# Self attention in a decoder kernel: another order of the steps in a turn

## Chip, cores and metric

The kernel runs on one core of a Trainium2 chip. The metric is the device time of one execution in microseconds (us). A core has five engines with a queue each, worked off in order: TensorE (PE; its weight loads are shown as PEld), VectorE (DVE), ScalarE (ACT), GpSimd (POOL) and SyncE (SP), which here issues most of the transfers. An instruction that waits for another engine holds up what stands behind it on its own queue.

## The reference

The program computes a two-layer decoder on x of shape 16 x 112 x 512 (batches, positions, width) in float32. It has seven stages: an attention, a quantized self attention joined with a quantized cross attention, a mixture of experts, a second attention, a second cross attention and a gated feed-forward layer. The change lies in the quantized self attention. Of its part of the reference, this is what matters (cut):

```python
ln_out = _ln(hidden_states, ln_w, ln_b)
q = _fp8_linear_pertensor(ln_out, wq, wq_scale, q_in_scale)   # 16 heads of 128
q = _ln(q, qln_w, qln_b)
k = _ln(_fp8_linear_pertensor(ln_out, wk, wk_scale, k_in_scale), kln_w, kln_b)  # 8 of 128
v = _fp8_linear_pertensor(ln_out, wv, wv_scale, v_in_scale)
core = _gqa(q, k, v)            # softmax(q k^T / sqrt(128)) v, two query heads to a key head
...
catq = _div_clamp_fp8(cat, proj_smooth)
out = einsum(catq, wproj) * (proj_in_scale * proj_w_scale)
```

`_fp8_linear_pertensor` scales and rounds its input to 8-bit floats before the product; `_div_clamp_fp8` does the same with the attention's output.

## The kernel before, in words

The stage is `stage_fp8_self` (line 888). The heads are worked through in four quarters q (four query heads and two key heads each). A unit (`SelfUnit`, line 736) is one quarter of one batch b; there are 4 x 16 = 64 units, in the order of `self_order` (line 875): first quarter 0 mixed with quarter 1, then 2 and 3. The tokens are stored in tiles of 128 rows while a batch has 112 positions, so 14 tiles cover 16 batches: units with b = 7 and b = 15 have no tile of their own, and so no queries and no keys to project (8 units in all).

A unit goes through its steps over several turns. `turn(n)` (line 920) runs, for different units, one step of each:

- `project_q` (750) of unit n: eight matmuls into ps_q, squares on ScalarE (L745), their sum on VectorE (L746).
- `project_kv` (761) of unit n: keys and values into ps_kv, squares of the keys, a copy of the values on ScalarE (L770), then on GpSimd the reciprocal root of the variance (`rsqrt`, L491 and L492), and on VectorE the products qk (L777), which free ps_q and ps_kv.
- `transpose` (782) of unit n-1: six transposes of qk into ps_t (L792), copied on ScalarE to qt and kt by batch (L485).
- `scores` (795) of unit n-2: ps_s (L799) and the extreme of each row on VectorE (L805).
- `exponentials` (807) of unit n-2: four exponentials with their sums on ScalarE (L812), a reciprocal on VectorE (L816) and the division on GpSimd (L817), which gives pr.
- `transpose_probs` (819) of unit n-3: four transposes of pr into ps_pt (L823), copied to pt on ScalarE (L825).
- `values` (827) of unit n-3: ps_av (L831), then scaled on VectorE (L856) and rounded by `round_fp8` (L504, L505, L506, L508 on VectorE, L510 on GpSimd), which gives r_o.
- `output` (837) of unit n-4: eight matmuls into ps_acc (L648), added to the residual x on VectorE (L872).

For quarter 0 the turn also quantizes the rows of unit n+2 (`Quantized`, line 654): `transpose` (L154) into ps_xt, `scale` (L679), which makes 16 scaled pieces on ScalarE in portions, and `rounded` (L687), which rounds the queries' and keys' inputs to xq (1024 wide, L504 to L510) and the values' inputs to xv (512 wide), and writes both to memory for the later quarters (L693, L703). Other quarters load them back two turns ahead (`quantized`, 707). At a turn's end come the loads of new rows (L440), one or two pieces of later weights (`Weights.step`, 549: a load L588, centring on VectorE L572, L578, L579, scaling and copying on ScalarE L600, L601, a remainder on GpSimd L602), and in 14 turns of quarter 2 to 3 `quantize_cross` (718), four more roundings of 512 columns on VectorE and one on GpSimd. In turns -2 to 4 some products of the next stage (`EarlyKeys.product`, L637) stand at the head of the turn.

TensorE and ScalarE run in the order in which the code calls the steps (`manual_schedule`, line 967); the other queues are put in order by the scheduler of the tile framework. PSUM has three buffers "mm" for ps_q and ps_kv, one "tr" for ps_xt, and four "sc" that ps_pt, ps_t (two), ps_s, ps_acc and ps_av take in turn, in the order in which they are asked for.

Of the kernel before, what the change touches and what calls it, by code (L numbers as in the profile page):

```python
# [9 lines left out]
F32 = mybir.dt.float32  # L10
F32R = mybir.dt.float32r
# [9 lines left out]
P = 128  # L21
# [4 lines left out]
KC = D // P  # L26
# [39 lines left out]
def batches_of(t):  # L66

    b, s = divmod(t * P, S)
    return [(b, s, 0, S - s), (b + 1, 0, S - s, P - S + s)]
# [366 lines left out]
def from_positions(k, dst, src, t):  # L436

    src = src.rearrange("(s b) d -> b s d", b=B)
    for b, s, r, n in batches_of(t):
        k.nc.sync.dma_start(out=dst[r : r + n], in_=src[b, s : s + n])  # L440
# [56 lines left out]
def round_fp8(k, wk, y, parts, tag="r8"):  # L497

    nc = k.nc
    m = wk.tile(list(y.shape), BF16, tag=f"{tag}_m", name="r8_m", bufs=2)
    t = wk.tile(list(y.shape), BF16, tag=f"{tag}_t", name="r8_t", bufs=2)
    nc.vector.tensor_scalar(y, y, FP8_MAX, -FP8_MAX, ALU.min, ALU.max)  # L504
    nc.vector.tensor_scalar(m.bitcast(U16), y.bitcast(U16), 0x7F80, None, ALU.bitwise_and)  # L505
    nc.vector.tensor_scalar(m, m, 2.0**-6, 1.5 * 2.0**4, ALU.max, ALU.mult)  # L506

    nc.vector.tensor_tensor(t, y, m, ALU.add)  # L508
    for dst, tok in parts:
        nc.gpsimd.tensor_tensor(dst, t[:, :, tok], m[:, :, tok], ALU.subtract)  # L510
# [143 lines left out]
class Quantized:  # L654
# [29 lines left out]
        if self.done == 4 * KC:  # L684
            k.nc.sync.dma_start(out=k.yx_dram[self.t], in_=y)

    def rounded(self):  # L687
        k, wk = self.k, self.wk
        xq = wk.tile([P, 2, KC, P], F32R, tag="xq", name="xq", bufs=3)
        round_fp8(  # L690
            k, wk, self.y[0], [(xq.rearrange("p v c s -> p (v c) s"), slice(0, P))], "q8"
        )
        k.nc.sync.dma_start(out=k.xq_dram[self.t], in_=xq.bitcast(F32))  # L693
        parts, full = [], []
        for b, s, r, n in batches_of(self.t):
            if s == 0:
                self.xv[b] = wk.tile([P, KC, S], F32R, tag="xv", name="xv", bufs=4)
            parts.append((self.xv[b][:, :, s : s + n], slice(r, r + n)))
            if s + n == S:
                full.append(b)  # L700
        round_fp8(k, wk, self.y[1], parts, "q8")
        for b in full:
            k.nc.sync.dma_start(out=k.xv_dram[b], in_=self.xv[b].bitcast(F32))  # L703
        return xq


def quantized(k, wk, b, xv):

    xq, t = None, tile_of(b)
    if t is not None:  # L710
        xq = wk.tile([P, 2, KC, P], F32R, tag="xq", name="xq", bufs=3)
        k.nc.sync.dma_start(out=xq.bitcast(F32), in_=k.xq_dram[t])
    xv[b] = wk.tile([P, KC, S], F32R, tag="xv", name="xv", bufs=4)
    k.last_load = k.nc.sync.dma_start(out=xv[b].bitcast(F32), in_=k.xv_dram[b])
    return xq


def quantize_cross(k, wk, t):

    y = wk.tile([P, KC, P], BF16, tag="r8_y", name="r8_y", bufs=2)  # L720
    k.nc.sync.dma_start(out=y, in_=k.yx_dram[t])
    xq = wk.tile([P, 2 * KC, P], BF16, tag="y_0", name="xqx", bufs=1)
    xq = xq.rearrange("p c s -> p (c s)").bitcast(F32).rearrange("p (c s) -> p c s", c=KC)
    round_fp8(k, wk, y, [(xq, slice(0, P))])
    k.nc.sync.dma_start(out=k.xx_dram[t], in_=xq)
# [149 lines left out]
def self_order():  # L875


    order, then = [], 0
    for b in range(B):
        order.append((0, b))  # L880
        while then < (b - 7) * 11 // 8:
            order.append((1, then))
            then += 1
    order += [(1, b) for b in range(then, B)]
    return order + [(q, b) for q in (2, 3) for b in range(B)]


def stage_fp8_self(k):

    nc = k.nc
    with k.stage("s2a", mm=3, tr=1, sc=4) as wk:
        order = self_order()
        total = len(order)
        heads, xv = [Heads() for _ in range(4)], [{} for _ in range(4)]
        units = [SelfUnit(k, wk, q, b, heads[q]) for q, b in order]
        inputs = {
            n: Quantized(k, wk, units[n].tile, xv[0])
            for n, (q, b) in enumerate(order) if q == 0 and units[n].tile is not None  # L900
        }
        weights = k.next_w + [Weights(k, "self", q, wk, raw=2) for q in (1, 2, 3)]
        weights.append(Weights(k, "cross", 0, wk, raw=2))
        last = [order.index((q, B - 1)) for q in range(4)]

        def at(n):
            return units[n] if 0 <= n < total else None


        early = {-2: 3, -1: 2, 0: 2, 1: 2, 2: 3, 3: 2, 4: 2}  # L910
        then = list(range(B))

        def products(count):
            for b in then[:count]:
                if b % GB == 2 and b // GB + 2 < NB:
                    k.early.load(b // GB + 2)
                k.early.product(b)
            del then[:count]

        def turn(n):  # L920
            new = inputs.get(n + 2)
            products(early.get(n, 0))
            if new:
                new.transpose()
                new.scale(5)
            if at(n):
                units[n].project_q(weights[order[n][0]], xq.pop(n))
            if new:
                new.scale(5)
            if at(n):  # L930
                units[n].project_kv(xv[order[n][0]].pop(order[n][1]))
            if at(n - 3):
                units[n - 3].transpose_probs()
            if at(n - 1):
                units[n - 1].transpose()
            if at(n - 2):
                units[n - 2].scores()
            if new:
                new.scale(6)
            if at(n - 2):  # L940
                units[n - 2].exponentials()
            if at(n - 4):
                units[n - 4].output()
            if at(n - 3):
                units[n - 3].values()
            if new:
                xq[n + 2] = new.rounded()
            elif at(n + 2):
                q, b = order[n + 2]
                xq[n + 2] = quantized(k, wk, b, xv[q]) if q else None  # L950
            if n + 3 in inputs:
                inputs[n + 3].load()
            if 0 <= n < TILES:
                from_positions(k, k.x[:, n], k.x_dram, n)
            if n >= 3:
                weights[1].step(2)
            for q in range(3):

                if n >= last[q]:
                    count = 2 if q == 0 else 1  # L960
                    weights[q + 2].step(count, 3 if n >= last[q] + 4 else 1 + (q < 2))
            if at(n - 4) and order[n - 4][0] == 2 and units[n - 4].tile is not None:
                quantize_cross(k, wk, units[n - 4].tile)

        xq = {}
        inputs[0].load()
        with k.tc.manual_schedule(engines={mybir.EngineType.PE, mybir.EngineType.Activation}):
            for n in range(-2, total):
                turn(n)
        for n in range(total, total + 4):  # L970
            turn(n)
        k.next_w = weights[-1]
# [947 lines left out]
```

## Time and profile before

| what | value |
|---|---|
| median of 3 runs | 3947.13 us (3946.97 to 3949.84) |
| profiled execution | 3949.88 us, its span from the first to the last instruction 3948.2 us |
| mean granted clock of TensorE | 0.968 |
| busy TensorE, VectorE, ScalarE, GpSimd | 92%, 45%, 37%, 24% of the span |
| the stage of the change, first ps_xt (L154) to last ps_acc (L648) | about 296 to 1013 us |
| one ps_q group (L648, 8 matmuls 128x512) | 2.2 us |
| one exponential (L812, 112x112) | 358 ns, four a unit |
| one division (L817, 112x448, GpSimd) | 943 ns |
| the power in `rsqrt` (L492, 128x6, GpSimd) | 1341 ns |
| one copy of q or k by batch (L485) | 585 and 481 ns, two of each a unit |

In the views of a profile, a row names the line, the engine and the operation, then output<-input by the program's names. Tables of waits give in total the time that an engine stood before instructions of a line, how often, the longest, and which instruction ended the wait. In a timeline, the first number is the start in us from the span's start, the second the duration, and a bracket holds the idle time ahead of it and what ended that. The granted clock (PEclk) is the share of full speed at which TensorE was let run.

### The profile page before, as it was taken

Reading aid. Unit: us, or ns where it says so; the run is one execution under the profiler, and the core shown is the slowest. Engines: PE = TensorE matmul, PEld = TensorE weight load, DVE = VectorE, ACT = ScalarE, POOL = GpSimd, SP = SyncE. Lnnn points to the kernel's source line nnn. Section 1 sums busy time; section 2 is a strip of 40 time slices with the busy share of each in tenths; the row PEclk is TensorE's granted clock in tenths of the full one; section 3 lists DMA queues with packets and bytes.
Section 4 is the critical chain, followed back from the end, with each engine's and each line's share of the span. In section 5 each row is a group of like instructions: output and inputs, shape, how many; then the busy total and the mean of one; then the engine's idle time right before and its main releaser. Section 6 shows DMA issues by size and latency. Waiting matters only on the chain.

```text
span 3948.2 us, 46306 instructions
## 1 busy us (share of the span) xinstructions
PE 3649.8 (92%) x16482; PEld 2360.2 (60%) x16482; DVE 1781.3 (45%) x3856; ACT 1462.3 (37%) x4189; POOL 940.2 (24%) x1322
## 2 busy tenths in 40 slices
PE   7888788778799999999999999999989989999999
PEld 4445677667566566666666654555444445556788
DVE  4445767776545544454445553111243343214333
ACT  2546665445444444444444431111113341112222
POOL 2334545544322322232222220000123220000000
PEclk8999899999999999999999999999999999999999
DMA  2125323332211211121121113999930013122000
GB/s 75 56 101 173 102 91 101 113 116 88 74 56 54 73 50 50 47 72 45 51 79 48 45 35 114 296 319 317 307 124 11 1 30 118 63 71 88 11 11 17
DMA packets 118118, 364.56 MB, mean 92 GB/s; under 512 B 13280, under 2 KB 33248, under 8 KB 108848
## 3 DMA queue, kind: packets, MB, share of 16 engines
q1 hardware_dynamic: 105504, 332.20, 25.8%
q0 software_dynamic: 5040, 16.52, 1.1%
q10 hardware_dynamic: 7344, 12.89, 0.9%
q8 instruction: 131, 2.15, 0.2%
q14 instruction: 99, 0.81, 0.1%
HBM read 317.09 MB, written 44.47 MB: 92 GB/s over the span
## 4 chain that ended last, share of the span: by engine, by line
PE 67%; DVE 8%; POOL 5%; ACT 3%; issue 3%; DMA 2%; SPq 0%; ACTq 0%; POOLq 0%; DVEq 0%
PE ps_kv L1036 14%; PE ps L1385 5%; PE ps_av L1089 4%; PE ps_s L1064 3%; PE ps_y L1403 3%; PE ps_acc L648 3%; PE ps_u L1740 3%; PE ps_o L341 3%; PE ps_g L1740 3%; PE ps_q L1491 3%; PE ps_o L1722 3%; PE ps_p L1584 3%; PE ps_q L648 2%; PE ps_pt L1079 2%; PE ps L1340 2%
## 5 line engine op out<-in xcount | busy, mean ns | idle before, releaser
L1036 PE MATMUL ps_kv<-w_kv,ct 128*125 128x512 f32 x1408 | 637.4, 592 | 0.0
L1036 PEld LDWEIGHTS ps_kv<-w_kv,ct 128*125 128x125 f32 x1408 | 261.2, 187 | 277.2 <-issue 242.0
L510 POOL TENSOR_TENSOR r_o<-r_t,r_m 128x64 fp32r<-128x64 bf16 (+6 forms) x224 | 147.5, 676 | 435.7 <-DVE r_t L508 408.8
L980 ACT ACTIVATE pr<-ps_s,ex_m 112x375 f32<-112x375 f32 (+1 forms) x272 | 157.4, 579 | 161.9 <-DVE ex_m L979 151.7
L1385 PE MATMUL ps<-w_expert,xgt 128*128 128x448 f32 x560 | 216.4, 539 | 0.7 <-ACT xgt L1377 0.7
L1012 DVE TENSOR_REDUCE cu_v<-sq 125x2 f32<-125x256 f32 (+1 forms) x248 | 118.5, 478 | 181.2 <-ACT sq L1011 180.8
L233 POOL TENSOR_TENSOR pr<-pr,nq_s 112x448 f32<-112x448 f32 (+1 forms) x120 | 119.4, 996 | 323.9 <-DVE nq_s L232 249.3
L492 POOL TENSOR_TENSOR cu_v<-cu_v,mhalf 125x2 f32<-125x2 f32 (+1 forms) x248 | 190.0, 766 | 20.6
L228 ACT ACTIVATE pr<-ps_s,nq_m 112x112 f32<-112x112 f32 (+1 forms) x480 | 167.3, 373 | 58.9 <-DVE nq_m L220 54.6
L491 POOL TENSOR_SCALAR cu_v<-cu_v 125x2 f32<-125x2 f32 (+1 forms) x248 | 48.0, 194 | 581.3 <-DVE cu_v L1012 578.4
L1064 PE MATMUL ps_s<-kt,qt 128*112 128x375 f32 x512 | 183.1, 479 | 1.2 <-ACT pr L980 0.8
L979 DVE TENSOR_REDUCE ex_m<-ps_s 112x1 f32<-112x375 f32 (+1 forms) x272 | 148.5, 546 | 69.9 <-PE ps_s L1611 67.3
L1011 ACT ACTIVATE sq<-ps_kv 125x256 f32<-125x256 f32 x176 | 67.4, 383 | 272.6 <-PE ps_kv L1036 219.9
L485 ACT ACTIVATE qt<-ps_t,turned 128x448 f32<-128x448 f32 (+6 forms) x224 | 116.5, 572 | 137.9 <-PE ps_t L1048 127.3
L1089 PE MATMUL ps_av<-pt,vn 125*128 125x224 f32 x768 | 162.4, 362 | 0.0
L1385 PEld LDWEIGHTS ps<-w_expert,xgt 128*128 128x128 f32 x560 | 103.7, 190 | 91.9 <-issue 91.0
L648 PE MATMUL ps_acc<-w_self,r_o 128*128 128x512 f32 x448 | 130.0, 436 | 28.8 <-POOL r_o L510 23.6
L1079 PEld LDWEIGHTS ps_pt<-ident,pr 112*125 112x125 f32 x768 | 102.8, 189 | 89.5 <-DVE pr L1071 50.0
L242 ACT COPY ptt<-ps_pt 112x448 f32<-112x448 f32 (+1 forms) x120 | 67.3, 561 | 226.4 <-PE ps_pt L240 226.4
L1089 PEld LDWEIGHTS ps_av<-pt,vn 125*128 125x128 f32 x768 | 145.3, 194 | 8.7 <-ACT pt L1082 3.9
L1064 PEld LDWEIGHTS ps_s<-kt,qt 128*112 128x112 f32 x512 | 90.1, 177 | 99.7 <-issue 59.7
L1079 PE MATMUL ps_pt<-ident,pr 112*125 112x112 f32 x768 | 118.4, 284 | 32.4 <-DVE pr L1071 30.5
(294 smaller groups left out, 7478.2 us busy)
## 6 DMA issues: line engine op xcount, KB each, us to landing
w_expert<-in_moe_w SPq DMA_DIRECT2D x105, 896.0 KB
ct<-in_ctx_t SPq DMA_DIRECT2D x64, 750.0 KB
xq<-xq_dram SPq DMA_DIRECT2D x42, 512.0 KB
xq<-xx_dram SPq DMA_DIRECT2D x56, 256.0 KB
raw<-in_self_w SPq DMA_DIRECT2D x48, 256.0 KB
w_sum<-in_ffn_w SPq DMA_DIRECT2D x12, 1024.0 KB
cn<-in_ctx SPq DMA_DIRECT2D x16, 750.0 KB
xv<-xv_dram SPq DMA_DIRECT2D x48, 224.0 KB
```

The costliest lines, as they stand in the source:

```text
L228: nc.scalar.activation(pr[:, j, :], self.ps[:, j, r * t : (r + 1) * t], AF.Exp, bias=self.mx[r][:, j : j + 1], scale=-1.0, accum_out=sums[ ...
L492: nc.gpsimd.tensor_tensor(dst, dst, bc(k.minus_half[: dst.shape[0]], [dst.shape[0], n]), ALU.pow)
L510: nc.gpsimd.tensor_tensor(dst, t[:, :, tok], m[:, :, tok], ALU.subtract)
L648: k.nc.tensor.matmul(out, lhs(c), w[i][:, c, :], start=first and c == 0 and i == 0, stop=last and c == n - 1 and i == 1,)
L979: nc.vector.tensor_reduce(mx, src, AX.X, ALU.min)
L980: nc.scalar.activation(dst, src, AF.Exp, bias=mx, scale=-1.0, accum_out=sums)
L1036: nc.tensor.matmul(pkv, self.ct[:, c, ch * CC : (ch + 1) * CC], w[:, c, :], start=c == 0, stop=c == KC - 1,)
L1064: nc.tensor.matmul(ps, self.heads.qt[self.b][:, h, :], self.kt[:, h // 2, :], start=True, stop=True)
L1079: nc.tensor.transpose(ps[:, h, :], self.pr[:, h, ch * CC : (ch + 1) * CC], k.ident[:S, :S])
L1089: nc.tensor.matmul(av[:, 2 * g : 2 * g + 2, :], self.vn[:, ch, g, :], self.pt[:, ch, 2 * g : 2 * g + 2, :], start=ch == 0, stop=ch == NCH - 1,
L1385: nc.tensor.matmul(pp, self.xt[:, c, :], w[:, c, :], start=c == 0, stop=c == 3)
L1740: nc.tensor.matmul(pp, w[:, c, cols], xt[:, part, c, :], start=c == 0 and part == 0, stop=c == 3 and part == 1,)
```

## The change

The same steps are called in another order within a turn, and `rounded` is cut into `round_qk` and `round_v`, so that the queries' and keys' inputs are rounded before the values and output steps and the values' inputs at the end. The transpose of new rows comes behind the queries and the scores; all scaling comes behind the exponentials.

Before: new rows' transpose, scaling, queries, scaling, keys and values, probabilities' transposes (n-3), transposes of q and k (n-1), scores (n-2), scaling, exponentials (n-2), output (n-4), values (n-3), rounding.

After: queries, scores (n-2), new rows' transpose, probabilities' transposes (n-3), exponentials (n-2), scaling, keys and values, scaling, rounding of xq, values (n-3), output (n-4), transposes of q and k (n-1), scaling, rounding of xv.

```diff
-    def rounded(self):
+    def round_qk(self):
         k, wk = self.k, self.wk
-        xq = wk.tile([P, 2, KC, P], F32R, tag="xq", name="xq", bufs=3)
-        round_fp8(
-            k, wk, self.y[0], [(xq.rearrange("p v c s -> p (v c) s"), slice(0, P))], "q8"
-        )
-        k.nc.sync.dma_start(out=k.xq_dram[self.t], in_=xq.bitcast(F32))
-        parts, full = [], []
+        self.xq = wk.tile([P, 2, KC, P], F32R, tag="xq", name="xq", bufs=3)
+        to = self.xq.rearrange("p v c s -> p (v c) s")
+        round_fp8(k, wk, self.y[0], [(to, slice(0, P))], "q8")
+        k.nc.sync.dma_start(out=k.xq_dram[self.t], in_=self.xq.bitcast(F32))
+
+    def round_v(self):
+        k, wk, parts, full = self.k, self.wk, [], []
...
-        return xq
...
             products(early.get(n, 0))
+            if at(n):
+                units[n].project_q(weights[order[n][0]], xq.pop(n))
+            if at(n - 2):
+                units[n - 2].scores()
             if new:
                 new.transpose()
-                new.scale(5)
-            if at(n):
-                units[n].project_q(weights[order[n][0]], xq.pop(n))
+            if at(n - 3):
+                units[n - 3].transpose_probs()
+            if at(n - 2):
+                units[n - 2].exponentials()
             if new:
                 new.scale(5)
             if at(n):
                 units[n].project_kv(xv[order[n][0]].pop(order[n][1]))
+            if new:
+                new.scale(5)
+                new.round_qk()
             if at(n - 3):
-                units[n - 3].transpose_probs()
+                units[n - 3].values()
+            if at(n - 4):
+                units[n - 4].output()
             if at(n - 1):
                 units[n - 1].transpose()
-            if at(n - 2):
-                units[n - 2].scores()
             if new:
                 new.scale(6)
-            if at(n - 2):
-                units[n - 2].exponentials()
-            if at(n - 4):
-                units[n - 4].output()
-            if at(n - 3):
-                units[n - 3].values()
-            if new:
-                xq[n + 2] = new.rounded()
+                new.round_v()
+                xq[n + 2] = new.xq
```

## The prediction

> **What bounds the kernel now.** I read the page first: TensorE is busy for 92% of the span, so only time in which it stands can be won cheaply. The change touches one stage, the quantized self attention, which the rows of its projections and outputs place between about 296 and 1013 us. So next came TensorE's waits in that window, then busy time and granted clock of its two halves, and then the timeline of single turns.
>
> TensorE's waits, 300 to 1013 us (us in total, times, longest):
> ```profile
> engine line waited for: us in total, times, longest us
> PE ps_pt L823 <- POOL pr L817: 86.6, 35, 6.1
> PE ps_acc L648 <- POOL r_o L510: 23.6, 16, 3.3
> PE ps_kv L648 <- DVE qk L777: 7.3, 9, 1.8
> PE ps_xt L154 <- DMA xn<-xn_dram: 6.4, 2, 3.8
> PE ps_acc L648 <- ACT pt L825: 4.7, 4, 2.2
> PE ps_av L831 <- ACT pt L825: 0.5, 1, 0.5
> ```
> The sum is 129 us, two thirds of it in the probabilities' transposes, which wait for GpSimd's division. The other 82% of the stage TensorE works. Busy time per engine with the clock, for the part in which rows are still quantized and the part after it:
> ```profile
> core 0: us, PE busy (x) PEld busy (x) DVE busy (x) ACT busy (x) POOL busy (x), PEclk, DMA share, GB/s
> 340.00:560.00 220.00, 182.76 (x1037) 154.80 (x1036) 149.12 (x317) 150.61 (x466) 114.88 (x126) 0.91 0.32 107
> 560.00:1013.00 453.00, 366.80 (x2214) 322.96 (x2214) 307.03 (x641) 222.67 (x737) 214.12 (x250) 0.94 0.30 99
> ```
> No other engine is full (VectorE 68%). What delays the division is a ring of in-order queues. One turn of it in the timeline (start, duration, idle before in brackets):
> ```profile
> 785.41 1.32 POOL L492 TENSOR_TENSOR su_v<-su_v,mhalf 128x6 f32<-128x6 f32 x1
> 786.76 0.69 DVE L777 TENSOR_TENSOR qk<-ps_q,su_v 128x512 f32<-128x512 f32 x1 [2.52 <-POOL su_v L492]
> 787.70 0.61 DVE L805 TENSOR_REDUCE su_m<-ps_s 112x4 f32<-112x448 f32 x1
> 788.41 0.35 ACT L812 ACTIVATE pr<-ps_s,su_m 112x112 f32<-112x112 f32 x1 [5.57 <-DVE su_m L805]
> 789.89 0.18 DVE L816 RECIPROCAL su_s<-su_s 112x4 f32<-112x4 f32 x1 [0.98 <-ACT pr L812]
> 790.21 0.93 POOL L817 TENSOR_TENSOR pr<-pr,su_s 112x448 f32<-112x448 f32 x1 [3.48 <-PE ps_kv L648]
> 791.20 0.60 PE L823 MATMUL ps_pt<-ident,pr 112*112 112x112 f32 x4 [1.09 <-POOL pr L817]
> ...
> 796.90 1.32 POOL L492 TENSOR_TENSOR su_v<-su_v,mhalf 128x6 f32<-128x6 f32 x1
> ```
> The maximum of the scores (L805) was computable long before, but it stands on VectorE behind the product qk (L777), which waits for GpSimd's power (L492), which needs the squares, which stand on ScalarE behind the exponentials that wait for the maximum. The ring closes after 796.90 - 785.41 = 11.5 us; TensorE's own pieces need less. From the rows around 930 us, without a wait: queries 2.02, keys and values 1.88, probabilities' transposes 0.38, transposes of q and k 0.66, scores 0.72, output 1.94, values 0.59, together 8.19 us.
>
> In a turn without queries (8 of 64) the transposes come sooner after the last turn's division and the wait is longest, and the group behind it runs slow:
> ```profile
> 748.70 0.99 PE L823 MATMUL ps_pt<-ident,pr 112*112 112x112 f32 x4 [5.10 <-POOL pr L817]
> ```
>
> **What the change does, part by part.** It adds and removes no arithmetic, and TensorE's 8.19 us a turn stay. It moves pieces. Laid end to end in the new order a turn is: queries 0 to 2.02, scores to 2.74, probabilities' transposes to 3.12, keys and values to 5.00, values to 5.59, output to 7.53, transposes to 8.19.
>
> *The ring.* In the program as built, VectorE's queue in a turn after the quantizing is: variance sum of q, maximum, reciprocal, variance sum of k, r_y, qk twice, then the rounding of the values with the residual x (L872) in it. Its loop from the durations in the rows: variance 0.60, maximum 0.61, then 1.58 from the maximum's end to the reciprocal (788.31 to 789.89) is 2.8; division 0.32 later for 0.93 is 4.05; L491 and L492 with 0.29 and 1.32 is 5.7; qk pair 0.94 is 6.65; L504 0.25, x 0.60, L505, L506, L508 0.31, 0.31, 0.39 is 8.5 us. So 8.5 against 8.19: nearly TensorE's pace, where it is 8.5 to 11.5 now. The power still waits on VectorE for 2 us or so, but the maximum and the exponentials are no longer queued behind it.
>
> *Who is late next.* The loop starts when the first squares are done, 2.9 us into the turn. The division ends 4.05 later, at 6.95; it is used at 8.19 + 2.74 = 10.93, 4 us of margin. x ends at 2.9 + 7.5 = 10.4; it frees the PSUM buffer that the next turn's probabilities' transposes take (four "sc" buffers, six uses a turn, and the output lies four uses before), so 0.5 us of margin: this is the new tight place. The values' r_o ends at 12.6 and is used by the output at 13.8: 1.2 us. The reordered output, behind the values, gains that margin.
>
> *The added wait.* Scores now follow the transposes of q and k with only the queries between; before, a whole turn lay between. Behind the waiting scores in TensorE's queue stands the whole turn. The copies out (L485, at 932.12 and 933.03, 1.05 and 0.83 us) end 1.85 us after the transposes' last piece; the queries last 2.02, so they just cover it. Without queries nothing covers: 8 turns x 1.8 = 14 us of new stall, in place of 31.7 us that these turns wait for the division today (1.9 to 5.3 each).
>
> *Weight pieces.* Centring a raw piece on VectorE (L572, L578, L579: 0.69 + 0.30 + 0.64) and the copies on ScalarE (0.62, or 0.73 + 0.62) come once or twice a turn. Part of the centring falls into the 1.6 us wait for the exponentials. What does not fit pushes x past its 0.5 us; I allow 10 us over the stage (below: 0 if all fit; above: 28 centrings x 0.9 = 25).
>
> *Cross quantization in 14 turns.* L504 to L508 at 512 wide add 1.5 us on VectorE, and sometimes wait for r_o on GpSimd: loops of 8.7 to 10.9, mean 9.7, so 14 x 1.5 = 21 us remain (0 to 38).
>
> *round_qk and round_v.* The same instructions, cut in two, with their two transfers on SP's queue in the same order. The transpose of new rows moves behind the queries, so their load has 2 us more; about 4 of 6.4 us remain. Later transfers on SP (weights, xq two turns ahead) have some 16 us of cover; I cost them at nothing, and a late one would cost its own lateness. Where the queries' rounding goes is where a rule speaks against the change. The row: a 448-wide L505 takes 0.28 us alone (940.00) and 1.30 beside GpSimd's L602 (791.31). The Trainium skill, "SBUF — State Buffer", section "SBUF: two separate sides", says that the two engines share a port pair under an exclusive lock, so the later one blocks fully. Queries are now rounded ahead of the values, and GpSimd's xq pass takes 2.18 us: by the rule up to 14 x 2.2 = 31 us on the chain to r_o. In the built queues r_o stands ahead of xq, so the lock hits the 512-wide ops of round_v instead, as it does now (L504 2.20 us at 414.82). I add none of the 31. The rounding turns still need some 19.3 us a pair (13.8 with rounding, 5.5 after it, much of whose work is then done) against 17 on TensorE: with the heavy weight turns about 24 us remain of 43.
>
> *Drain.* The last outputs wait 2.2 + 2.8 + 3.3 us for r_o; nothing changes there: 8 us remain.
>
> Remaining waits: 14 + 10 + 21 + 24 + 4 + 8 = 81 of 129; saved 48 us.
>
> *The clock.* At 0.91 and 0.94, throttling costs 182.8 x 0.09 + 366.8 x 0.06 = 38 us of the busy time. The group of four transposes takes 0.60 after waits up to 2.24 us and 0.87 to 1.00 after 2.56 or more. The Trainium skill, "TensorE: Matmul & The Clock Gate", Part 1, puts the idle window that halves the clock at about 3.4 us: by the rule only the nine waits over 3.4 count, each with some 1.7 us lost (one window at half rate, an estimate), 15 us; by the rows all 38 could come back if no wait over 2.5 stays. Stalls of 1.8 us would be harmless by both. I take half of the rows' sum, 19 us.
>
> Sum: 48 + 19 = 67. The profiled execution took 3949.9 us (span 3948.2), so 3883; the median of the runs lies 2.8 below it, so 3880.
>
> **Rivals.**
> *TensorE waits for next to nothing.* If weights, cross quantization and rounding all hide, only 14 + 8 + 4 = 26 us remain: 103 saved and 30 of clock give 3947 - 133 = 3814. For it: no engine is over 68% busy. Against: the loop is 8.5 even without the extras. Chance 0.15.
> *VectorE's loop stays the pace-maker.* With x and rounding behind qk the loop is as long as before, 9.5 to 10, and only the no-query turns win: 32 - 14 = 18, so 3929; if it takes back more, within 0.2%. For it: the 0.5 us of margin at x. Chance 0.13, nearly half of it within 0.2% (about 8 us, all that a measurement of this kernel tells from no change).
> *Slower: scores wait for keys every turn.* L799 waits for L485 if ScalarE comes late. The margin is 0.2 us; 56 turns with queries pay all beyond it. It outweighs my 67 us once ScalarE is late by 0.2 + 1.2 = 1.4 us in every turn; at 2 us late it costs 56 x 1.8 = 101, so 3947 - 67 + 101 = 3981. For it: in the 14 turns with new rows five scalings of 0.37 us stand ahead of the copies. Against: ScalarE is busy 49% after 560 us, and the weight copies of up to 2.7 us come behind. Chance 0.12.
> That the queues ignore the new order is excluded for TensorE and ScalarE (written by hand), and the built VectorE queue shows the maximum ahead of qk.
>
> **How the numbers follow.** The forecast has 0.60. Its own spread is 3845 to 3915, from the bounds above (weights, cross quantization, clock). Faster: 0.60 + 0.15 + 0.07 = 0.82; within: 0.06; slower: 0.12. The range runs from just under the first rival to just over no change, 3810 to 3948.
>
> **What would show it.** Right: L823's wait for L817 under 15 us; L805 no longer behind L777; new waits of L823 for x (L872) and of L799 for L485, the latter near 1.8 us in eight turns; clock above 0.95 after 560 us. Wrong: L799 waiting in turns with queries; L823 waiting over 40 us in sum; the clock unmoved though waits are gone.

## The result, and the profile after

The changed kernel takes 3905.1 us (median of 4 runs, 3901.9 to 3907.7) against 3948.5 us on the same chip: a ratio of 0.9885, with a 95% interval of 0.9867 to 0.9902. The forecast was 3880 in a range of 3810 to 3948; it named the direction and overrated the size by half (67 us against 43). The profiled execution has a span of 3901.9 us, 46.3 less than before.

TensorE's waits in the stage (300 to 968 us) as they stand now, in the columns of the first view of the prediction:

```profile
engine line waited for: us in total, times, longest us
PE ps_s L799 <- ACT kt L485: 25.3, 17, 4.2
PE ps_pt L823 <- DVE x L872: 23.5, 16, 2.6
PE ps_kv L648 <- DVE qk L777: 15.1, 11, 4.2
PE ps_av L831 <- ACT pt L825: 10.6, 9, 2.5
PE ps_t L792 <- ACT pr L812: 8.5, 8, 1.8
PE ps_acc L648 <- POOL r_o L510: 4.8, 3, 3.2
PE ps_xt L154 <- DMA xn<-xn_dram: 4.5, 2, 3.4
PE ps_t L792 <- DVE r_y L856: 2.0, 1, 2.0
PE ps_pt L823 <- POOL pr L817: 0.5, 2, 0.3
```

The wait that made up two thirds of the old sum, L823 for the division, is gone: 86.6 us have become 0.5. The output's wait for r_o has shrunk too, from 23.6 us to 4.8. In their place stand smaller ones, for the keys' copies, x, qk, pt and the exponentials; the sum is 95 us where it was 129.

Busy time and granted clock of the two halves; the stage now ends at 965.7 us, where it ended at 1013.8:

```profile
340.00:560.00 220.00, 187.58 (x1069) 157.94 (x1068) 161.20 (x333) 155.02 (x487) 120.03 (x132) 0.92 0.33 109
560.00:966.00 406.00, 346.83 (x2177) 304.64 (x2176) 264.18 (x626) 218.70 (x711) 207.43 (x244) 0.98 0.34 110
```

For the same matmuls TensorE is busy 534.4 us, 15 less than the 549.6 before, and the granted clock went from 0.94 to 0.98 after 560 us. 34 us of waits and 15 of busy time make up the 48 us of the stage; 2 us are given back later.

One turn of the ring now (start, duration):

```profile
927.09 0.62 DVE L805 TENSOR_REDUCE su_m<-ps_s 112x4 f32<-112x448 f32 x1
927.79 0.36 ACT L812 ACTIVATE pr<-ps_s,su_m 112x112 f32<-112x112 f32 x1 [2.36 <-DVE su_m L805]
...
929.28 0.18 DVE L816 RECIPROCAL su_s<-su_s 112x4 f32<-112x4 f32 x1 [1.58 <-ACT pr L812]
929.60 0.93 POOL L817 TENSOR_TENSOR pr<-pr,su_s 112x448 f32<-112x448 f32 x1 [1.78 <-DVE su_s L816]
930.79 1.32 POOL L492 TENSOR_TENSOR su_v<-su_v,mhalf 128x6 f32<-128x6 f32 x1
932.15 0.69 DVE L777 TENSOR_TENSOR qk<-ps_q,su_v 128x512 f32<-128x512 f32 x1 [1.64 <-POOL su_v L492]
...
933.27 0.68 DVE L872 TENSOR_TENSOR x<-x,ps_acc 128x512 f32<-128x512 f32 x1
934.10 0.57 PE L823 MATMUL ps_pt<-ident,pr 112*112 112x112 f32 x4 [0.99 <-DVE x L872]
935.39 0.62 DVE L805 TENSOR_REDUCE su_m<-ps_s 112x4 f32<-112x448 f32 x1
```

The maximum (L805) now runs 5 us ahead of qk (L777), and the division is done at 930.5, 2.6 us before TensorE comes to L823 (at 933.1, where its wait begins). From one maximum to the next it is 935.39 - 927.09 = 8.3 us. This is one turn, close to the 8.5 us that the prediction gave VectorE's loop, but also to the 8.19 it gave TensorE, so it does not tell which of the two sets the pace. What L823 waits for instead is x, which stands behind qk and frees a PSUM buffer.

Where the time came from, by stretch (units counted from 0; from the start of one unit's value projection, the second half of ps_kv, to another's; the drain, in which the last units finish and no new one starts, is from the last unit's to the first matmul of the next stage; all us, from one profiled execution each):

| kernel | to unit 21 | 21 to 36 | 36 to 50 | 50 to 63 | drain | stage end |
|---|---|---|---|---|---|---|
| before | 561.6 | 152.9 | 144.9 | 118.0 | 36.4 | 1013.8 |
| changed | 556.0 | 140.7 | 133.1 | 112.9 | 23.0 | 965.7 |
| scores alone (first experiment) | 553.9 | 136.4 | 134.2 | 108.6 | 32.0 | 965.2 |
| values first alone (second) | 560.8 | 149.6 | 140.1 | 111.1 | 26.3 | 987.8 |
| both, before's other order (eighth) | 557.7 | 148.2 | 142.5 | 112.0 | 23.0 | 983.4 |
| scores, and values first in the drain (twelfth) | 549.2 | 134.4 | 132.8 | 108.7 | 22.9 | 948.0 |

Of the 48 us, 6 lie in the part up to unit 21, in which rows are quantized, 24 in units 21 to 50, 5 in 50 to 63, and 13 in the drain, for which the prediction had nothing. How far single executions vary shows in the first and the twelfth experiment: their order is the same up to unit 63, and yet they lie 4.7 us apart at unit 21 and 8.1 at unit 63. So the 6 us of the first part are hardly more than that variation, while the drain takes 22.9 or 23.0 us in three of these runs.

### The profile page after: what moved, and what is told of

Same layout as the page of the kernel before. It is cut to its first block, busy times and chain, and to the rows that moved or that the text cites. A ratio compares the mean times of both kernels' runs of the same rounds, so it can differ in the third digit from the quotient of the medians.

```text
span 3901.9 us, 46406 instructions
## 1 busy us (share of the span) xinstructions
PE 3637.8 (93%) x16482; PEld 2347.2 (60%) x16482; DVE 1750.9 (45%) x3856; ACT 1465.7 (38%) x4189; POOL 938.1 (24%) x1322
## 4 chain that ended last, share of the span: by engine, by line
PE 68%; DVE 8%; POOL 5%; issue 4%; ACT 3%; DMA 3%; SPq 0%; POOLq 0%; ACTq 0%; DVEq 0%
PE ps_kv L1038 14%; PE ps L1387 5%; PE ps_av L1091 4%; PE ps_s L1066 3%; PE ps_y L1405 3%; PE ps_acc L648 3%; PE ps_u L1742 3%; PE ps_o L341 3%; PE ps_g L1742 3%; PE ps_o L1724 3%; PE ps_q L1493 3%; PE ps_q L648 3%; PE ps_p L1586 3%; PE ps_pt L1081 2%; PE ps_v L1508 1%
## 5 line engine op out<-in xcount | busy, mean ns | idle before, releaser
L510 POOL TENSOR_TENSOR r_o<-r_t,r_m 128x64 fp32r<-128x64 bf16 (+6 forms) x224 | 148.2, 679 | 483.1 <-DVE r_t L508 459.8
L491 POOL TENSOR_SCALAR cu_v<-cu_v 125x2 f32<-125x2 f32 (+1 forms) x248 | 48.0, 194 | 580.1 <-DVE cu_v L1014 577.3
L856 DVE TENSOR_TENSOR r_y<-ps_av,r_smooth 128x448 bf16<-128x448 f32 x128 | 79.3, 620 | 145.7 <-PE ps_av L1091 129.6
```

## The experiments

The theory: the maximum queued behind qk closed a ring over VectorE, ScalarE and GpSimd, and what the change gains is the opening of that ring. The rivals: the position of pieces on TensorE (output behind values), the split of the rounding, or a pace that VectorE's work sets anyway.

**Scores alone.** The kernel before, with two calls moved:

```diff
                 units[n].project_q(weights[order[n][0]], xq.pop(n))
+            if at(n - 2):
+                units[n - 2].scores()
...
                 units[n - 3].transpose_probs()
+            if at(n - 2):
+                units[n - 2].exponentials()
             if at(n - 1):
                 units[n - 1].transpose()
-            if at(n - 2):
-                units[n - 2].scores()
...
-            if at(n - 2):
-                units[n - 2].exponentials()
```

> The kernel before with one move: scores (n-2) behind the queries, exponentials behind the probabilities' transposes. Ring theory (the maximum queued behind qk is what cost the time): the maximum gets ahead of qk, so L823's wait for L817 falls from 87 us to under 25 and most of the change's 43 us comes back, 3900 to 3920. Rival (the gain needs the whole order, above all the output behind the values): under 12 us gained, 3936 or more. Output now asks for the PSUM buffer of the same turn's scores, so a new wait of L648 (ps_acc) for the exponentials, up to 0.6 us a turn, is possible.

Measured: 3895.6 us, ratio 0.9847 (0.9813 to 0.9881). Its waits:

```profile
PE ps_acc L648 <- POOL r_o L510: 40.2, 29, 5.0
PE ps_acc L648 <- ACT pt L825: 13.5, 13, 8.5
...
PE ps_pt L823 <- POOL pr L817: 1.4, 1, 1.4
```

The wait for the division falls to 1.4 us. These two moves alone bring at least as much as the whole change. The theory holds for its main point, and the time is a little better than the 3900 to 3920 it said. The price is on the first line: the output, ahead of values, waits 40.2 us for r_o where it waited 23.6.

**Values first alone.** The kernel before with `values` called ahead of `output`.

> The kernel before with one move: values ahead of output. Ring theory: the ring stays, L823 still waits over 70 us for L817; at most part of the 24 us that the output waits for r_o goes, 3935 to 3948. Rival (output's margin is what counts): 25 us or more gained, under 3923.

Measured: 3925.5 us, ratio 0.9940 (0.9911 to 0.9969).

```profile
PE ps_pt L823 <- POOL pr L817: 83.9, 36, 6.9
...
PE ps_acc L648 <- POOL r_o L510: 1.4, 1, 1.4
```

The ring's wait stays, as expected, but the time falls by 24 us, more than I had expected and just short of the rival: the output's wait for r_o goes from 23.6 to 1.4 us, and although values now wait 10.7 us for pt, most of it comes back as time. So it was not hidden by the ring, it stood beside it. And 10 of the stage's 26 us are the drain (36.4 to 26.3). So the ring is the larger cause, not the only one.

**The maximum left out.** The kernel before; `scores` makes no maximum, and the exponentials use a constant.

```diff
-        self.mx = k.small.tile([S, 4], F32, tag="su_m", name="su_m")
-        nc.vector.tensor_reduce(self.mx, ps, AX.X, ALU.min)
...
-                self.pr[:, h, :], self.ps[:, h, :], AF.Exp, bias=self.mx[:, h : h + 1],
+                self.pr[:, h, :], self.ps[:, h, :], AF.Exp, bias=k.minus_half[:S, 0:1],
```

> The kernel before without the maximum of the scores (L805): the exponentials use a constant in its place, so this part of the softmax is left out. It cuts the ring at one point and leaves every other step where it was. Ring theory: the squares no longer wait for VectorE's product, L823's wait for L817 falls from 87 us to under 35 and the kernel gains 25 to 50 us, 3898 to 3923. It also takes 40 us of work from VectorE. Rival (positions on TensorE's queue decide): L823 waits over 60 us, gain under 15 us.

Measured: 3898.6 us, ratio 0.9879 (0.9865 to 0.9893). The lines missing from this kernel shift the numbers: L821 is the old L823, L815 the old L817.

```profile
PE ps_pt L821 <- POOL pr L815: 47.6, 19, 5.9
```

**The power left out.** The kernel before; in `project_kv` only L491 of `rsqrt` remains.

> The kernel before without the power L492 in the self units (the variance is used as it is; this part of the normalization is left out). It takes 1.35 us out of the ring in 56 turns. Ring theory: in the 30 or so turns where the ring and not TensorE sets the pace, 1.35 us each come back: 25 to 50 us, 3898 to 3923. Rival: a wait beside others, gain under 10 us.

Measured: 3890.5 us, ratio 0.9855 (0.9840 to 0.9869).

```profile
PE ps_pt L823 <- POOL pr L817: 53.8, 27, 5.8
```

Both cut or shorten the ring without moving a piece on TensorE, and both gain as much as the change or more, some 50 and 58 us, the second more than the 25 to 50 expected. In it, 1.35 us were taken from 56 units, 76 us in all; the gain is three quarters of that. Each also takes work away, 40 us from VectorE and 76 from GpSimd; it is the run with the scores alone moved, which removes no work, that shows the order to be enough. The wait for the division falls less than I had said, to 48 us without the maximum, where it was to be under 35, and to 54 without the power. In part this is the eight turns without queries, in which TensorE has little of its own and comes too soon: 23 of the 48 and 21 of the 54 us lie there (31.7 of the 86.6 before). The rest stays unexplained.

**Rounding joined again.** The changed kernel with `round_qk` called just ahead of `round_v`.

> The changed kernel with both roundings together at the end of the turn again. My prediction cost the split at nothing: within 8 us of the changed kernel, 3897 to 3913. Rival (the split earns part of the gain in the first third, where rows are quantized): 3915 or more, with the added waits before 560 us.

Measured: 3893.9 us, ratio 0.9840 (0.9805 to 0.9875); its profiled span is 3901.8 us against 3901.9 for the changed kernel, and unit 21 comes at 554.5 against 556.0. The median is 3 us below the range I had stated. The split earns nothing. Whether it costs a few us the runs do not tell: the medians lie 11 us apart, but the intervals overlap and the profiled spans agree.

**Output in another PSUM buffer.** The changed kernel; in turns without new rows the output's product goes to the idle buffer "tr".

```diff
-                units[n - 4].output()
+                units[n - 4].output(None if new else "tr")
```

> The changed kernel with the output's product in the PSUM buffer of the row transposes in turns that have no new rows, so that the residual x no longer holds one of the four buffers that the probabilities' transposes need. If that buffer is the wait that took the ring's place: L823's 23.5 us of waiting for x go to about 3, and 12 to 25 us are gained, 3880 to 3893. Rival (VectorE's loop itself paces these turns): the wait comes back at r_o or qk with nearly the same sum, 3898 to 3908.

Measured: 3904.5 us, ratio 0.9877 (0.9847 to 0.9908). After 560 us:

```profile
PE ps_s L799 <- ACT kt L485: 24.9, 17, 4.0
PE ps_kv L648 <- DVE qk L777: 13.2, 18, 2.6
PE ps_acc L648 <- POOL r_o L510: 12.0, 12, 2.3
```

The 23.5 us behind x are gone, and most of them are back at the keys' copies, qk and r_o (9.9, 8.6 and 1.6 us there in the changed kernel). The rival's forecast came true: the buffer was only the last to come. In the first third the new rows' transposes now waited 12.8 us for x, a wait that the changed kernel does not have; the stage ends 8 us later in this execution, no more than two executions of one order may differ.

**The same, and in turns without queries the values' projection ahead of the scores:**

> The kernel with the output in the row transposes' buffer, and in the 8 turns without queries the values' projection (1 us) ahead of the scores, so that it covers part of the copies that the scores wait for. If the eight turns each pay 1 us less at L799, L799's wait for L485 falls by 8 to 12 us and the kernel gains 5 to 12 us on the one without it. Rival: these turns have slack on TensorE anyway and the wait moves to the next piece: within 4 us.

Measured: 3905.3 us, ratio 0.9901 (0.9880 to 0.9923), within its intervals no gain on the one without it. L799's wait for the keys fell from 32.9 to 27.8 us and L831's for pt rose from 7.4 to 14.8.

**Both moves in the old order.** The kernel before with the scores and exponentials early and values ahead of output.

> The kernel before with both moves: scores and exponentials early, values ahead of output; transposes of q and k stay in the middle of the turn. If the two gains seen alone add where they lie in different places (turns for the scores, the drain and r_o for the values), the output's 40 us of waiting for r_o in the run with the scores alone falls under 12, the drain is 10 us shorter, and the kernel takes 3865 to 3885. Rival (one pace-maker behind both, as the moves together in the changed kernel suggest): 3893 to 3908.

Measured: 3912.1 us, ratio 0.9915 (0.9890 to 0.9939), 17 us slower than the scores alone and above both ranges that were expected.

```profile
PE ps_acc L648 <- ACT pr L812: 23.1, 9, 3.9
PE ps_av L831 <- ACT pt L825: 14.5, 13, 4.0
PE ps_acc L648 <- DVE r_y L856: 10.6, 2, 6.6
```

The two gains do not add. With six uses of four "sc" buffers each order hands each piece another predecessor, and here output seems to take over, in nine turns, a buffer that exponentials still read: at 734.67 it starts 0.2 us after the last of the four ends. **With the output in "tr"** that wait goes:

> The same, with the output's product in the row transposes' PSUM buffer in turns without new rows. If x still holds a buffer that TensorE needs, 5 to 15 us are gained on the kernel with both moves; rival (as in the changed kernel, where this earned nothing): within 5 us.

Measured: 3909.6 us, ratio 0.9896 (0.9880 to 0.9913). Units 21 to 50 take 270.7 us where they took 290.7, so those 20 us were the buffers; but up to unit 21 it loses 13, with 33.8 us of waiting of the new rows' transposes for x. On the whole it is within 5 us of the eighth, as the rival had it.

**Transposes of q and k back ahead of values**, in the changed kernel:

> The changed kernel with the transposes of q and k put back ahead of values and output. If moving them to the end of the turn cost the changed kernel what it lacks against the run with the scores alone: L799's wait for L485 falls from 25 us to under 8, and the kernel gains 10 to 25 us, 3880 to 3895. Rival (the wait only shows what VectorE's loop takes anyway): within 5 us of the changed kernel, the waits moving to r_o or x.

Measured: 3901.9 us, ratio 0.9878 (0.9862 to 0.9894), no different from the changed kernel.

```profile
PE ps_acc L648 <- ACT pr L812: 23.3, 11, 3.0
PE ps_s L799 <- ACT kt L485: 21.1, 11, 4.8
```

The scores' wait for the keys fell by 4 us only: after 560 us from 9.9 to 1.5, but before it rose from 15.4 to 19.6, and the output waits for the exponentials as in the eighth. Moving these transposes back gains nothing; and what the changed kernel lacks against the scores alone, 10 us by the medians, is itself not clear of the intervals.

**Output ahead of values**, in the changed kernel:

> The changed kernel with output ahead of values again. If values ahead of output is worth the drain: the stretch from the last keys-and-values group to the next stage grows from 23 us to 32 or more, and the kernel loses 8 to 20 us, 3913 to 3925. Rival (the swap counts only where the ring paces): within 5 us.

Measured: 3924.8 us, ratio 0.9943 (0.9926 to 0.9959); the drain takes 31.7 us, the output waits 33.4 us for r_o, and the scores wait 30.6 for x, since the buffers change hands with the order. The swap is worth some 20 us in the changed kernel, 9 of them in the drain.

**Scores alone, and values first only in the drain.** The first experiment with one line in two places:

```diff
+            if n >= total - 1 and at(n - 3):
+                units[n - 3].values()
             if at(n - 4):
                 units[n - 4].output()
-            if at(n - 3):
+            if n < total - 1 and at(n - 3):
                 units[n - 3].values()
```

> The kernel with the scores and exponentials alone moved, and values ahead of output only in the last turn with new work and the four after it, where nothing else is left for TensorE. If the two effects lie in different stretches: turns as in the run with the scores alone (last keys and values near 933 us), the stretch from there to the next stage 22 to 25 us in place of 32, and 8 to 10 us under that run, 3884 to 3892, the fastest of all. Rival (the drain's end is set by the chain of the last unit alone): 30 us or more for the stretch, within 4 us of the run with the scores alone.

Measured: 3886.2 us, ratio 0.9838 (0.9823 to 0.9852), the lowest median here, 62 us under before. Against before it is not told apart from the scores alone (0.9847) or the joined rounding (0.9840), but its drain takes 22.9 us against 32.0 in the first, and these 9 us are the difference of the two medians. The last keys and values came at 925.1 and not 933, 8 us earlier than in the first experiment; up to there the two orders are the same, so that part is variation between executions. Why the drain was long shows in the last outputs of the kernel before, and in those of the twelfth:

```profile
996.49 2.12 PE L648 MATMUL ps_acc<-w_self,r_o 128*128 128x512 f32 x8 [2.19 <-POOL r_o L510]
...
1002.50 3.66 PE L648 MATMUL ps_acc<-w_self,r_o 128*128 128x512 f32 x8 [2.75 <-POOL r_o L510]
...
1010.17 3.78 PE L648 MATMUL ps_acc<-w_self,r_o 128*128 128x512 f32 x8 [3.26 <-POOL r_o L510]
```

```profile
938.12 2.15 PE L648 MATMUL ps_acc<-w_self,r_o 128*128 128x512 f32 x8
...
942.43 2.19 PE L648 MATMUL ps_acc<-w_self,r_o 128*128 128x512 f32 x8
946.01 2.11 PE L648 MATMUL ps_acc<-w_self,r_o 128*128 128x512 f32 x8 [1.39 <-POOL r_o L510]
```

In the old order a unit's values stand in the queue behind the output that waits for the rounding of the unit before; so each rounding starts only when the last one has been used, and the last groups take 3.7 us in place of 2.1. With values first the rounding of one unit runs beside the output of another. The granted clock of the drain goes with it, from 0.85 in the kernel before to 1.00 in the changed one:

```profile
977.40:1013.70 36.30, 24.37 (x112) 19.67 (x111) 15.72 (x38) 9.88 (x41) 9.45 (x13) 0.85 0.00 1
942.70:965.60 22.90, 18.16 (x101) 14.85 (x100) 14.09 (x32) 8.38 (x33) 8.53 (x12) 1.00 0.01 1
```

The four turns of the drain are called outside `manual_schedule`; TensorE's rows there keep the order of the calls all the same.

## Why the prediction was right, and where its sizes were off

- **The ring: right, and shown.** L823's wait for L817 fell from 86.6 to 0.5 us; moving the scores and exponentials alone does it, and so, in part, does taking the maximum or the power out where they stand.
- **Remaining waits: 81 us forecast, 95 measured.** Up to 560 us they fell only from 43.6 to 36.8, where the forecast had some 32 (24 for the rounding turns, 4 for the load, 4 for two turns without queries); from there to the last unit's values from 73.8 to 54.0, where the terms for weights, cross quantization and the other six turns without queries make some 42; in the drain from 11.8 to 4.7, where it had 8.
- **Scores behind the keys' copies.** The term for the eight turns without queries was right: 14 us forecast, 11.0 measured, 1.2 in most of them. But L799's wait is 25.3 us in all: 1.2 lie in the drain, and 13.1 in eight turns with queries, which the forecast had at nothing because the queries just cover the copies. Up to 560 us these waits reach 4.2 us; before the one at 382.80, ScalarE works through two portions of five scalings of new rows before it comes to the copies. I had named that queue only in the slower rival, and "L799 waiting in turns with queries" as a sign of being wrong: it came, in eight turns of 56.
- **Weights and cross quantization:** 10 + 21 = 31 us forecast. That they ended up at x, the exponentials' buffer and r_y, which together took 23.5 + 8.5 + 2.0 = 34, is likely but not shown. The place of x, with the least margin, was right; that a seat elsewhere would not help (the output in another buffer) was not foreseen.
- **qk:** the keys' and values' wait for qk rose from 7.3 to 15.1 us; I had no term for it.
- **The drain: the step that was wrong.** "Nothing changes there" did not hold: the output's waits of 2.2, 2.8 and 3.3 us became one of 1.4, since the order of values and output sets how the last units overlap. The stretch fell from 36.4 to 23.0 us, 7 of them waits and 6 busy time. Without this gain of 13 us the time would have been near 3918, so a part of the measured 43 us was luck.
- **The clock:** 19 us forecast; TensorE's busy time fell by 15, 6 of them in the drain. After 560 us the granted clock rose as forecast; before, it only went from 0.91 to 0.92. Six waits over 2.5 us remain there (nine before), but the tenth and twelfth experiments have six such waits too and a clock of 0.95, so why it stayed is open. (The nine waits over 3.4 us of the prediction are those of L823; with the load's 3.78 they are ten, and four remain.) With 8 of 17 waits over 2.5 us left in the stage, the 15 us do not decide between the two sizes that the prediction weighed.
- **round_qk and round_v at nothing:** no gain from the split; a small cost stays open. GpSimd's pass over xq falls on round_v, as foreseen: at 385.56 its 512-wide L505 takes 2.12 us beside xq's 2.60 (from 384.92), with r_o done before. No sign of the 31 us that the prediction weighed and left out: with the roundings joined again the stage ends at 966.9 us, against 965.7.
- **Rivals.** Scores late in every turn did not come about. That TensorE would wait for next to nothing was wrong too.
- **Open:** what paces units 21 to 63 at some 379 to 388 us in the changed kernel, with the scores alone, with the output in another buffer, and in the ninth and tenth experiments. Waits trade places there when a buffer or a piece is moved, so one loop over several engines is likely, but no run isolates it. A hint: without the maximum the stretch took 368.6 us and without the power 375.1, in the old order, so work on VectorE or GpSimd may still count there.

## What to carry to other kernels

When the longest wait in a stage points at one engine, follow it over the in-order queues: an instruction that was ready long ago but stands behind one that waits can close a ring, and moving that one step can be worth as much as a whole new order. Count the drain of a software pipeline (steps of several units overlapped in one loop) on its own; here TensorE had nothing else to do there, and waits and slow groups went straight into the time. And when several steps share a few buffers in the order of asking, recompute who follows whom for every new order, since two gains that each hold alone may cost each other.

## What the runs showed of the hardware

Nothing new but a size. The first three rows are of the changed kernel, the last of the first experiment:

```profile
526.05 1.76 PE L799 MATMUL ps_s<-kt,qt 128*112 128x112 f32 x8 [1.93 <-ACT kt L485]
722.15 0.44 PE L792 MATMUL ps_t<-ident,qk 128*128 128x128 f32 x2 [1.64 <-ACT pr L812]
723.90 1.66 PE L799 MATMUL ps_s<-kt,qt 128*112 128x112 f32 x8 [1.32 <-ACT kt L485]
615.57 1.04 PE L799 MATMUL ps_s<-kt,qt 128*112 128x112 f32 x8 [2.65 <-ACT kt L485]
```

A scores group takes 0.95 us without a wait and 1.04 after one of 1.2. It took 1.76 after a wait of 1.93, and 1.66 after two of 1.64 and 1.32 with 0.44 us of work between, but only 1.04 after one of 2.65. In the trace before, the probabilities' transposes kept their pace after 2.24 us. So the length of the last wait alone does not decide whether a group runs slow; what does, no run isolates. The prediction took stalls of 1.8 us as harmless, and some not much longer were not.
